# A shorter inverse root, a two-part transpose of z and two redistributed quarters of values in a hybrid attention and FFN kernel

## The chip, the cores and the metric

The kernel runs on one core of one Trainium2 chip. The metric is the device time of one execution in microseconds (us). Engines are named as in the profile: PE (TensorE matmul), PEld (its weight loads), DVE (VectorE), ACT (ScalarE), POOL (GpSimd), SP (SyncE, which here only issues DMAs). All data are fp32. The trace shows most fp32 matmuls as two records each, transposes as one.

## The reference

The input x is four images of 512 x 256. Four residual blocks follow one another, each on a layer norm of x:

```python
x = x + attn_a(layernorm(x))   # window attention on 16-channel tokens
x = x + ffn(layernorm(x))      # 256 -> 2048 -> 256, gated, weights stored as 4-bit codes
x = x + attn_b(layernorm(x))   # causal attention, 16 heads of 16, rope
x = x + ffn(layernorm(x))      # the same FFN weights
```

`attn_a` has two branches of 8 channels, each with attention in windows of 8 tokens, plus a depthwise convolution of the values ("lepe"); the two are joined, projected, normalised over 16 channels (with a weight and a bias) and added to the tokens. `ffn` first decodes its weights (a table of 16 values, one scale per 32), then computes `down(gelu(gate(x)) * up(x))`.

## The kernel before

**The passes.** The work goes image by image. Image 0's window attention runs alone at the start (the startup). Then image 0's first FFN pass runs on PE while DVE does image 1's window attention and decodes the remaining FFN weights (the first slot, `first_slot`). Then the FFN pass of image 1 runs beside the window attention of image 2, that of image 2 beside image 3 (`weave` with `beside_window`). Image 3's first pass and the second FFN passes follow, beside the causal attention. An FFN pass is 64 matmuls of 512 columns into gate banks (`pg`, L893) and up banks (`pu`, L914) and 64 of 256 columns into output banks (`po`, L939). Each of 16 hidden chunks needs one DVE product `it` (L923 in the first slot) before its `po` matmuls; each finished `po` bank is added to X by DVE (L954).

**What sets the order.** Each engine executes its own queue in order and waits on semaphores. In the startup and the first slot the order of PE and DVE is the order in which the program is written out (in the startup also ACT and SP). In the first slot a planner (`Pace`) decides where the FFN matmuls go between the window work: it keeps two clocks, `pe` and `dve`. `spend(us)` adds to the DVE clock and lets PE take further FFN steps (0.88 us each, two matmuls) as long as the PE clock is behind; it also emits FFN products and adds that have come due. `matmuls(us)` adds window matmuls to the PE clock. The planner only knows these written costs. In the later images only PE's order is by hand; DVE's is the scheduler's.

**Names around the change.**
- `window_front`: loads image b as `xa`, takes the variance of 128 rows (L323, L326), averages it over two halves with a small matmul `pm` (L295), gets a power -0.5 on POOL (L334), scales `xa` (L347 DVE, L351 ACT), transposes it (`yTp`, L360; copied by ACT to `yT`, L367), and makes the matmuls `qkv` (L408), `taps` (L393) and `lepe` (L381), which ACT copies to `T` (L419, L425). For image 0, `busy(n)` puts n matmuls on PE whose results nobody reads (`idle`, L451), 8 before `pm` and 12 after it.
- `window_parts`: `products` and `weighted` make 128 x 2048 products on DVE (`tq`, L517; `tv`, L598, L608). `values_here` folds such a product on DVE in three steps and adds lepe (L621, L623). `values_piled` instead accumulates its 8 slices on PE with identity matmuls (`va`, L478), and `take_piled` copies the bank by ACT into `att` (L639). `halved` does the first fold on DVE (L485), so that only 4 slices are left to pile. The buffers of `tmp` are two.
- `window_back`: `project(hf)` transposes half of `att` (`aTp`, L696), ACT copies it to `aT` (L698, one buffer), PE projects it (L702), DVE adds the bias (`pr`, L705), scales it (`prw`, L709) and sums the squares (`ss`, L711). `turn()` calls `newton_root` (L97 to L102) on `ss` and makes the two halves of `z` (L721, L723). `move()` brings both halves of `z` to row layout with 64 small matmuls (`zp`, L741), and `add()` adds them to X (L752).
- `norm_rows` then takes the row statistics (L828 to L834), POOL's power (L835), the scaled rows `xn` (L846), their transposes `xTp` (L866) and ACT's copies to `xT` (L869), with which the image's FFN pass starts.
- `dequant` (driven as `words`) loads the packed codes and scales of 12 weight quarters (`pkg`, `sbg` and so on; L780 to L783) and decodes each in six DVE steps (L797 to L810). In the startup `next(words)` after the statistics of image 0 sets off the first load: DVE writes one column of `pkg` (L780), and SP, whose queue holds all later loads, starts after it.

Of the kernel before, what the change touches and what calls it, by code (L numbers as in the profile page):

```python
# [10 lines left out]
F32 = mybir.dt.float32  # L11
# [3 lines left out]
ALU = mybir.AluOpType  # L15
AX = mybir.AxisListType

P = 128
# [17 lines left out]
def hybrid_kernel(  # L36
# [34 lines left out]
    def pair(name):  # L71
        return side.tile([P, 2, 512], F32, tag="pair", name=name)
# [21 lines left out]

    def newton_root(y, var, t, scale):

        nc.vector.tensor_scalar(var, var, scale, EPS, ALU.mult, ALU.add)  # L97
        nc.vector.tensor_scalar(y.bitcast(I32), var.bitcast(I32), -0.5, float(0x5F3759DF), ALU.mult, ALU.add)
        for _ in range(3):
            nc.vector.tensor_tensor(t, y, y, ALU.mult)  # L100
            nc.vector.scalar_tensor_tensor(t, t, -0.5, var, ALU.mult, ALU.mult)
            nc.vector.scalar_tensor_tensor(y, t, 1.5, y, ALU.add, ALU.mult)  # L102

    class Pace:

# [179 lines left out]
    def window_front(a1, a2, c, b, y, state):  # L285
# [12 lines left out]
        if b in (1, 2):  # L298

            junk = a1.tile([P, P], F32, tag="junk", name=f"junka{b}")  # L300
            for s in range(8):
                if b == 2 and s == 4:
                    yield 2.5
                nc.scalar.activation(junk, y[:, s, :], AF.Identity, accum_out=mv[:, s, 0:1])
            yield 3.5
            ps = over_halves(0, mv[:, :, 0])
            nc.scalar.activation(mean, ps, AF.Copy, scale=-1.0 / P)
            yield 1.0
            for s in range(8):
                if b == 2 and s == 4:  # L310
                    yield 2.5
                nc.scalar.activation(
                    junk, y[:, s, :], AF.Square, bias=mean[:, s : s + 1], accum_out=mv[:, s, 1:2]
                )
            yield 3.5
            nc.scalar.activation(off, over_halves(1, mv[:, :, 1]), AF.Copy, scale=1.0 / P)
            inv_root(rs, off)
            nc.gpsimd.tensor_tensor(mean, mean, rs, ALU.mult)
            yield 3.0
        else:  # L320
            for s in range(8):
                st = a2.tile([P, 6], F32, tag="st", name=f"sta{b}_{s}")
                ins = nc.vector.bn_stats(st, y[:, s, :])  # L323
                if b == 3:
                    queue_behind(ins, state["f1"])
                nc.vector.bn_aggr(mv[:, s, :], st)  # L326
            yield 3.5
            if b == 0:
                busy(8)
            mm = over_halves(0, mv.rearrange("p s t -> p (s t)")).rearrange("p (s t) -> p s t", t=2)  # L330
            nc.vector.tensor_tensor(off, mv[:, :, 0], mm[:, :, 0], ALU.subtract)
            nc.vector.tensor_tensor(off, off, off, ALU.mult)
            nc.vector.scalar_tensor_tensor(off, off, EPS, mm[:, :, 1], ALU.add, ALU.add)
            nc.gpsimd.tensor_tensor(rs, off, mhalf, ALU.pow)  # L334

            yield 4.0
            yield 4.0
            behind = last_on(mybir.EngineType.DVE).name
            ins = nc.vector.scalar_tensor_tensor(mean, mm[:, :, 0], -1.0, rs, ALU.mult, ALU.mult)
            if b > 1:  # L340
                queue_behind(ins, behind)
# [339 lines left out]
    def window_back(a1, a2, c, b, state):  # L681


        y, att = state[b]
        attf = att.rearrange("p s j c -> p s (j c)")
        ss = a1.tile([P, 2, 32], F32, tag="ss", name=f"ss{b}")

        prs = a1.tile([P, 4, 8, 64], F32, tag="tmp", bufs=2, name=f"prw{b}")
        prs = [prs[:, 2 * hf].rearrange("p a n -> p (a n)").rearrange("p (n c) -> p n c", c=C) for hf in range(2)]

        def project(hf):
            n = f"{b}_{hf}"
            pss = pair(f"aTp{n}")
            ps = pss[:, 0, :]
            for s in range(4):
                nc.tensor.transpose(ps[:, s * P : (s + 1) * P], attf[:, 4 * hf + s], ident)  # L696
            aT = a1.tile([P, 4, P], F32, tag="aT", name=f"aT{n}")
            nc.scalar.copy(aT.rearrange("p s q -> p (s q)"), ps)  # L698
            yield 1.2
            ps = pss[:, 1, :]  # L700
            for s in range(4):
                nc.tensor.matmul(ps[:, s * P : (s + 1) * P], aT[:, s, :], c["pw"], start=True, stop=True)  # L702
            yield 0.0
            pr = a2.tile([P, 32, C], F32, tag="pr", name=f"pr{n}")
            nc.vector.tensor_tensor(pr, ps.rearrange("p (n c) -> p n c", c=C), bcast(c["pb"], 1, 32), ALU.add)  # L705
            paced(0.6)
            sq = a2.tile([P, 32, C], F32, tag="sq", name=f"sqa{n}")
            nc.scalar.activation(sq, pr, AF.Square)
            nc.vector.tensor_tensor(prs[hf], pr, bcast(c["lnw"], 1, 32), ALU.mult)  # L709
            paced(0.6)  # L710
            nc.vector.tensor_reduce(ss[:, hf], sq, AX.X, ALU.add)  # L711
            paced(0.6)
            yield 1.8

        def turn():
            root = a1.tile([P, 2, 64], F32, tag="root", name=f"root{b}")
            newton_root(root[:, 0], ss.rearrange("p a n -> p (a n)"), root[:, 1], 1.0 / C)
            zs = []
            for hf in range(2):
                pr = prs[hf]  # L720
                nc.vector.tensor_tensor(pr, pr, bcast(root[:, 0, 32 * hf : 32 * hf + 32], 2, C), ALU.mult)  # L721
                z = a2.tile([P, 4, 4, 4, 8], F32, tag="sq", name=f"z{b}_{hf}")
                ins = nc.vector.tensor_tensor(  # L723
                    z.rearrange("p c i s j -> p (s j) i c"),
                    pr.rearrange("p n (i c) -> p n i c", c=4),
                    y[:, 4 * hf : 4 * hf + 4].rearrange("p s (j i c) -> p (s j) i c", j=8, c=4),
                    ALU.add,
                )
                zs.append(z)
            state[b, "z"], state[b, "moved"] = zs, ins.ins.name  # L730
            yield 7.2

        def move():


            ps = state[b, "moving"] = pair(f"zp{b}")
            for hf in range(2):
                z = state[b, "z"][hf]
                for q in range(8):
                    for c4 in range(4):  # L740
                        nc.tensor.matmul(  # L741
                            ps[32 * c4 : 32 * c4 + 32, q // 4, (q % 4) * P : (q % 4 + 1) * P],
                            c["sel"][:, q, hf, :],
                            z[:, c4].rearrange("p i s j -> p (i s j)"),
                            start=hf == 0 and q % 4 == 0,
                            stop=hf == 1,
                            skip_group_check=True,
                        )

        def add():  # L750
            to = X[b].rearrange("p i (s q j) -> p (i s) q j", s=4, q=8)
            ins = nc.vector.tensor_tensor(  # L752
                to, to, state[b, "moving"].rearrange("p a n -> p (a n)").rearrange("p (q n j) -> p n q j", q=8, j=8), ALU.add
            )
            state["due"] = ins.ins.name

        return project, turn, move, add


# [548 lines left out]
    def drain(work):  # L1308
        for _ in work:
            pass  # L1310
# [37 lines left out]
    with ExitStack() as left:  # L1348
# [21 lines left out]
        with tc.manual_schedule(  # L1370
            engines={mybir.EngineType.PE, mybir.EngineType.DVE, mybir.EngineType.Activation, mybir.EngineType.SP}
        ):
            wconst = next(consts)
            front = window_front(a1, a2, wconst, 0, xa, state)
            next(front)
            next(words)
            next(consts)
            next(front)
            next(consts)
# [34 lines left out]
            next(ahead)  # L1414
            rows_shift(wconst, 0)
            w["weighted"](0, 1)
            w["lepe_first"](1)
            w["values_piled"](0, 1)
            w["total_here"](1)
# [25 lines left out]
            add()  # L1445
            busy(1, wconst["wide"])
            drain(ahead)
            busy(2, wconst["wide"])
            drain(norm_rows(f1, 0, "f0", got, aside=lambda: some(words, 3)))
            del state["due"]  # L1450

# [4 lines left out]
        def first_slot():  # L1456
# [45 lines left out]
            for br in range(2):  # L1502
# [4 lines left out]
                for hf in range(2):  # L1507
                    w["weighted"](br, hf)
                    if br == 0:
                        step()  # L1510
                    if (br, hf) == (1, 0):
                        w["values_piled"](br, hf, one("va1"))
                        run.matmuls(4.2)
                        w["take_piled"](br, (hf,))
                        continue
# [15 lines left out]
            run.matmuls(0.9)  # L1531
            drain(second)
            pieces(72 - made[0])
            drain(turn())
            run.spend(6.2)
            while run.steps < 89:
                run.spend(0.2)
            move()
            run.matmuls(3.8)
            run.spend(max(0.0, run.pe - run.dve))  # L1540
            add()
            run.spend(1.2)
# [154 lines left out]
```

## Time and profile before

| what | value |
|---|---|
| three runs, us | 1021.25, 1021.71, 1024.87 (median 1021.71) |
| the profiled execution, us | 1020.95 |
| its span, us (1.85 us lie around it) | 1019.1 |
| PE busy in the span | 1000.8 us (98%) |
| DVE busy | 672.2 us (66%) |
| ACT, POOL busy | 350.8 us, 128.1 us |
| startup: 0 to 72.9 us | PE busy 65.71 |
| first slot: 72.9 to 182.0 us | PE busy 103.89 |
| the rest: 182.0 to 1019.0 us | PE busy 831.17 |
| granted TensorE clock, mean | 0.996 |

The busy share of PE counts matmuls whose results nobody uses, and a matmul at half the clock counts twice as long. What PE waits for is read in two views: the timeline of PE, which puts idle time and what ended it in brackets behind a line, and the stretches, which give busy time and granted clock for any interval. Times there are us from the start of the span.

### The profile page before, as it was taken

What the parts mean: (1) busy time and instruction counts of PE and PEld (TensorE: products, weight loads), DVE (VectorE), ACT (ScalarE), POOL (GpSimd) and SP (SyncE); (2) the same over time, 40 slices, a digit from 0 to 9 for tenths busy, and PEclk for the clock granted to TensorE, in tenths of its full rate; (3) what the DMA queues carried; (4) which work ended last, traced back from release to release, by engine and by line L of the source; (5) the groups of instructions that cost most, each with busy time, mean ns of one, the idle gap of its engine ahead of it and who ended that gap; (6) DMA issues with size and microseconds to landing.
All of it is one profiled execution on the core that took longest, in us unless ns stands there. A gap on an engine that the chain in (4) does not pass through costs nothing.

```text
span 1019.1 us, 14265 instructions
## 1 busy us (share of the span) xinstructions
PE 1000.8 (98%) x5548; PEld 590.8 (58%) x5548; DVE 672.2 (66%) x1591; ACT 350.8 (34%) x606; POOL 128.1 (13%) x251
## 2 busy tenths in 40 slices
PE   8999998999999999999999999999999999999998
PEld 6864667465746575554574644754645746446556
DVE  8889998887948678756577554766466575652111
ACT  3463241133112223435424346145253253451110
POOL 2100000100000013012330112401113201120000
PEclk9999999899999999999999999999999999999999
DMA  5220100000000020000000000000000000000000
GB/s 148 85 62 23 62 22 22 0 1 1 1 1 0 2 68 1 1 1 1 1 2 0 2 1 1 6 16 1 1 1 1 21 1 2 1 1 21 0 1 21
DMA packets 14900, 15.32 MB, mean 15 GB/s; under 512 B 2866, under 2 KB 11338, under 8 KB 14802
## 3 DMA queue, kind: packets, MB, share of 16 engines
q1 hardware_dynamic: 12416, 13.31, 4.4%
q10 hardware_dynamic: 2322, 1.07, 0.5%
q8 instruction: 43, 0.70, 0.3%
q14 instruction: 23, 0.19, 0.1%
q0 software_dynamic: 96, 0.05, 0.0%
HBM read 12.32 MB, written 2.10 MB: 14 GB/s over the span
## 4 chain that ended last, share of the span: by engine, by line
PE 93%; DVE 4%; DMA 1%; POOL 0%; ACT 0%; issue 0%; POOLq 0%; SPq 0%; DVEq 0%; ACTq 0%
PE pg_s L893 11%; PE pg_f L893 11%; PE pu_s L914 11%; PE po_f L939 11%; PE pu_f L914 11%; PE po_s L939 11%; PE s L1103 5%; PE o L1188 4%; PE sT L1152 4%; PE qkv_b L1042 3%; PE va L478 1%; PE zp L741 1%; PE qkT L1079 1%; PE qkv_b L1046 1%; PE sc L478 1%; PE ob L1203 1%
## 5 line engine op out<-in xcount | busy, mean ns | idle before, releaser
L1118 DVE CUSTOM_DVE_ANT_0 junk<-s,mask 128x512 f32<-128x512 f32 (+3 forms) x256 | 110.1, 486 | 36.9 <-PE s L1103 19.8
L893 PE MATMUL pg_f<-xT_f,g 128*128 128x512 f32 x256 | 125.6, 606 | 1.4 <-ACT xT_f L869 1.3
L893 PE MATMUL pg_s<-xT_s,g 128*128 128x512 f32 x256 | 126.7, 603 | 0.0
L914 PE MATMUL pu_s<-xT_s,u 128*128 128x512 f32 x256 | 125.4, 601 | 0.0
L914 PE MATMUL pu_f<-xT_f,u 128*128 128x512 f32 x256 | 122.6, 596 | 0.0
L939 PE MATMUL po_s<-d,it_s 128*128 128x256 f32 x512 | 118.0, 382 | 0.0
L939 PE MATMUL po_f<-d,it_f 128*128 128x256 f32 x512 | 117.0, 381 | 0.0
L939 PEld LDWEIGHTS po_s<-d,it_s 128*128 128x128 f32 x512 | 95.2, 190 | 20.8 <-issue 8.8
L939 PEld LDWEIGHTS po_f<-d,it_f 128*128 128x128 f32 x512 | 95.2, 190 | 18.0 <-issue 5.6
L1168 POOL TENSOR_SCALAR_AFFINE_SELECT e<-e 128x256 f32<-128x256 f32 x128 | 52.5, 422 | 344.9 <-ACT e L1164 342.3
L1164 ACT ACTIVATE e<-sT 128x1024 f32<-128x1024 f32 (+1 forms) x72 | 66.4, 968 | 72.0 <-PE sT L1152 72.0
L914 PEld LDWEIGHTS pu_f<-xT_f,u 128*128 128x128 f32 x256 | 47.4, 191 | 55.1 <-issue 52.4
L893 PEld LDWEIGHTS pg_s<-xT_s,g 128*128 128x128 f32 x256 | 45.9, 190 | 56.8 <-issue 50.9
L893 PEld LDWEIGHTS pg_f<-xT_f,g 128*128 128x128 f32 x256 | 47.3, 192 | 54.2 <-issue 48.1
L914 PEld LDWEIGHTS pu_s<-xT_s,u 128*128 128x128 f32 x256 | 46.1, 190 | 54.4 <-issue 50.2
L905 ACT ACTIVATE gs_f<-pg_f 128x512 f32<-128x512 f32 x48 | 28.6, 596 | 128.7 <-PE pg_f L893 125.8
L902 DVE SCALAR_TENSOR_TENSOR g_s<-g_s,gs_s 128x512 f32<-128x512 f32 x48 | 33.2, 691 | 59.0 <-ACT g_s L901 58.5
L899 ACT COPY gs_s<-pg_s 128x512 f32<-128x512 f32 x48 | 28.1, 586 | 67.8 <-PE pg_s L893 67.5
L1103 PE MATMUL s<-kT,qT 16*128 16x384 f32 (+3 forms) x512 | 50.0, 467 | 0.0
L954 DVE TENSOR_TENSOR X<-po_s,X 128x256 f32<-128x256 f32 (+1 forms) x33 | 13.5, 412 | 54.0 <-PE po_s L939 54.0
L1188 PE MATMUL o<-e,V 128*32 128x256 f32 (+3 forms) x512 | 44.4, 441 | 0.3 <-PE sT L1152 0.3
L1103 PEld LDWEIGHTS s<-kT,qT 16*128 16x128 f32 x512 | 23.1, 183 | 32.5 <-issue 11.6
(236 smaller groups left out, 1348.6 us busy)
## 6 DMA issues: line engine op xcount, KB each, us to landing
X<-in_x_dram SPq DMA_DIRECT2D x4, 512.0 KB
out_dram<-X SPq DMA_DIRECT2D x15, 128.0 KB
xa<-in_x_dram SPq DMA_DIRECT2D x28, 64.0 KB
pkg<-in_gate_p_dram SPq DMA_DIRECT2D x4, 256.0 KB
sbg<-in_gate_s_dram SPq DMA_DIRECT2D x4, 256.0 KB
pku<-in_up_p_dram SPq DMA_DIRECT2D x4, 256.0 KB
sbu<-in_up_s_dram SPq DMA_DIRECT2D x4, 256.0 KB
pkd<-in_down_p_dram SPq DMA_DIRECT2D x4, 256.0 KB
```

The lines of the kernel that those rows point to most:

```text
L893: nc.tensor.matmul(pg, Wf["g"][par][q][:, o : o + P], xT[:, par, :], start=par == 0, stop=par == 1)
L902: nc.vector.scalar_tensor_tensor(g2, g2, 1.0, gs, ALU.add, ALU.mult)
L905: nc.scalar.activation(gs, pg, AF.Gelu_apprx_tanh)
L914: nc.tensor.matmul(pu, Wf["u"][par][q][:, o : o + P], xT[:, par, :], start=par == 0, stop=par == 1)
L939: nc.tensor.matmul(po[:, 0:W], inter[k][:, i * P : (i + 1) * P], Wf["d"][par][j // 2][:, (j % 2) * W : (j % 2 + 1) * W], start=k == 0, sto ...
L1042: nc.tensor.matmul(ps[:, 0, :], xT[:, par, rows], c["wqk"][:, :, par], start=par == 0, stop=par == 1)
L1103: nc.tensor.matmul(pss[hl // 2][:, hl % 2, at : at + n], qT[h0 : h0 + HD, g, i * P : (i + 1) * P], kT[h0 : h0 + HD, g, 0:n], start=True, s ...
L1118: nc.vector.tensor_tensor_reduce(out=junk[:, 0:n], in0=pss[k][:, hl % 2, at : at + n], in1=c["mask"][:, 512 - n : 512], scale=1.0, scalar= ...
L1152: nc.tensor.matmul(pss[hl // 2][:, hl % 2, at : at + n], kT[h0 : h0 + HD + 1, g, kt * P : (kt + 1) * P], qT[h0 : h0 + HD + 1, g, kt * P : ...
L1164: nc.scalar.activation(e[:, :, 0 : 512 - at0], pss[k][:, :, at0:512], AF.Exp)
L1168: nc.gpsimd.affine_select(out=diag, in_=diag, pattern=[[0, 2], [1, P]], compare_op=ALU.is_ge, fill=0.0, base=0, channel_multiplier=-1,)
L1188: nc.tensor.matmul(outs[g][h0 : h0 + 32, kt * P : 512], v[:, kt, 4 * g + hl, :], e[:, hl % 2, at : at + n], start=kt == 0, stop=kt == 2,)
```

## The change

Seven edits, in the order in which they take effect:

1. **Earlier first load.** Image 0's first `next(words)` (the one-column write and SP's load behind it) is put between the fourth and the fifth row statistic instead of behind all eight.
2. **Idle matmuls.** `busy(8)` ahead of `pm` becomes `busy(14)`; the last `busy(2)` of the startup becomes `busy(1)`.
3. **Startup values.** The product of branch 0, half 1 is halved by DVE, and PE piles 4 slices instead of 8.
4. **`aT` in two buffers.**
5. **`newton_root`.** The variance is scaled by 64/9 in the instruction that adds epsilon; after the bit-trick seed, one cubic step (four instructions) and one Newton step (three) replace three Newton steps of three instructions: nine instructions instead of eleven. All images use it.
6. **First slot, values.** Branch 0, half 0 of image 1 is no longer folded on DVE alone: DVE halves it, PE piles 4 slices and lepe, ACT copies the bank to `att`.
7. **First slot, z.** `turn()` yields after each half, and `move` takes the halves it is to move. In the first slot the program now reads: first half of z, `spend(4.0)`, move half 0, second half of z, `spend(1.8)`, move half 1. The rule that FFN step 89 had to be reached first is gone.

Edits 6 and 7 change the planner's clocks, so it puts the FFN matmuls elsewhere. In the queue of PE as built, the second matmul of the last up chunk and all of the second half's `po` matmuls come behind the projections of image 1: that `pu` matmul, 8 `po` of the first output bank, 4 of the second, the two halves of `zp` side by side, then 10 `po`, the first four `xTp`, 2 `po`, the other four `xTp` and 8 `po`. Before, PE made 8 of the 32 `po` matmuls around `yTp` and `qkv`, 18 between the projections and `zp`, and 6 behind `zp`. In DVE's queue the last product `it` (chunk 15), which stood behind `values_here` of half 0, now stands behind the first half of `z`; behind it comes the add of the first `po` bank, and then the second half of `z`.

```diff
     def newton_root(y, var, t, scale):
-        nc.vector.tensor_scalar(var, var, scale, EPS, ALU.mult, ALU.add)
+        over = 64.0 / 9.0
+        nc.vector.tensor_scalar(var, var, scale * over, EPS * over, ALU.mult, ALU.add)
         nc.vector.tensor_scalar(y.bitcast(I32), var.bitcast(I32), -0.5, float(0x5F3759DF), ALU.mult, ALU.add)
-        for _ in range(3):
-            nc.vector.tensor_tensor(t, y, y, ALU.mult)
-            nc.vector.scalar_tensor_tensor(t, t, -0.5, var, ALU.mult, ALU.mult)
-            nc.vector.scalar_tensor_tensor(y, t, 1.5, y, ALU.add, ALU.mult)
+        nc.vector.tensor_tensor(t, y, y, ALU.mult)
+        nc.vector.tensor_tensor(t, t, var, ALU.mult)
+        nc.vector.scalar_tensor_tensor(t, t, -10.0 / 3.0, t, ALU.add, ALU.mult)
+        nc.vector.scalar_tensor_tensor(y, t, 5.0, y, ALU.add, ALU.mult)
+        nc.vector.tensor_tensor(t, y, y, ALU.mult)
+        nc.vector.scalar_tensor_tensor(t, t, -0.5 / over, var, ALU.mult, ALU.mult)
+        nc.vector.scalar_tensor_tensor(y, t, 1.5, y, ALU.add, ALU.mult)
...
+                if b == 0 and s == 4:
+                    state["early"]()
                 ins = nc.vector.bn_stats(st, y[:, s, :])
...
-                busy(8)
+                busy(14)
...
-            aT = a1.tile([P, 4, P], F32, tag="aT", name=f"aT{n}")
+            aT = a2.tile([P, 4, P], F32, tag="aT", name=f"aT{n}")
...
+            state["early"] = lambda: next(words)
             next(front)
-            next(words)
...
             w["weighted"](0, 1)
+            w["halved"]("v", 0, 1)
             w["lepe_first"](1)
...
-            busy(2, wconst["wide"])
+            busy(1, wconst["wide"])
             drain(norm_rows(f1, 0, "f0", got, aside=lambda: some(words, 3)))
...
+                    if (br, hf) == (0, 0):
+                        w["halved"]("v", br, hf)
+                        w["values_piled"](br, hf, one("va0"))
+                        run.matmuls(2.4)
+                        w["take_piled"](br, (hf,))
+                        step()
+                        continue
...
-            drain(turn())
-            run.spend(6.2)
-            while run.steps < 89:
-                run.spend(0.2)
-            move()
-            run.matmuls(3.8)
+            turned = turn()
+            next(turned)
+            run.spend(4.0)
+            move((0,))
+            run.matmuls(1.9)
+            drain(turned)
+            run.spend(1.8)
+            move((1,))
+            run.matmuls(1.9)
```

## The prediction

> **What bounds the kernel now.** I read the head of the page and its chain first: PE is the bound.
>
> ```profile
> PE 1000.8 (98%) x5548; PEld 590.8 (58%) x5548; DVE 672.2 (66%) x1591; ACT 350.8 (34%) x606; POOL 128.1 (13%) x251
> PE 93%; DVE 4%; DMA 1%; POOL 0%; ACT 0%; issue 0%; POOLq 0%; SPq 0%; DVEq 0%; ACTq 0%
> ```
>
> Behind 182 us PE is busy 831.2 of 837.0 us, and its queue there stays the same. So the change can only act by the moment at which image 1's FFN pass starts (`pg_f` at 182.04), and by PE's clock around it. Next, the timeline of PE before that moment; brackets hold the idle time and what ended it.
>
> ```profile
> 157.78 0.66 PE L696 MATMUL aTp<-ident,att 128*128 128x128 f32 x4 [0.46 <-ACT att L639]
> 159.11 1.16 PE L702 MATMUL aTp<-pw,aT 128*128 128x128 f32 x8 [0.68 <-ACT aT L698]
> ...
> 161.44 1.16 PE L702 MATMUL aTp<-pw,aT 128*128 128x128 f32 x8 [0.73 <-ACT aT L698]
> 162.43 7.93 PE L939 MATMUL po_f<-d,it_f 128*128 128x256 f32 x36
> 170.29 3.70 PE L741 MATMUL zp<-z,sel 128*32 128x128 f32 x128
> 173.93 2.86 PE L939 MATMUL po_f<-d,it_f 128*128 128x256 f32 x12
> 179.43 1.94 PE L866 MATMUL xTp_f<-ident,xn_f 128*128 128x128 f32 x8 [2.65 <-DVE xn_f L846]
> 182.04 3.77 PE L893 MATMUL pg_f<-xT_f,g 128*128 128x512 f32 x4 [0.68 <-ACT xT_f L869]
> 185.62 1.91 PE L914 MATMUL pu_f<-xT_f,u 128*128 128x512 f32 x4
> ```
>
> PE idles 5.2 us here, 2.65 of it behind `zp`. The four `pg_f` records at 182.04 take 3.77 us, the four behind them 1.91: the stretches (busy us of PE, PEld, DVE, ACT, POOL, then granted clock, DMA share, GB/s) say why.
>
> ```profile
> 178.80:185.70 6.90, 5.60 (x13) 3.15 (x14) 6.10 (x11) 1.07 (x2) 0.04 (x1) 0.51 0.00 0
> ```
>
> The clock was halved for 6.9 us behind the 2.65 us pause. That cost 1.9 us in `pg_f` (3.77 against 1.88) and 0.6 in `xTp` (1.94 against 1.32 at 70.89): 2.5 us. In the timeline of DVE I look for the product `it_f` that the last `po` matmuls need, and for the way to z:
>
> ```profile
> 143.73 0.68 DVE L923 TENSOR_TENSOR it_f<-pu_f,gs_f 128x512 f32<-128x512 f32 x1
> ...
> 160.38 0.69 DVE L705 TENSOR_TENSOR pr<-aTp,pb 128x512 f32<-128x512 f32 x1 [1.02 <-PE aTp L702]
> ...
> 168.46 1.06 DVE L723 TENSOR_TENSOR z<-prw,xa 128x512 f32<-128x512 f32 x1
> ...
> 174.06 1.22 DVE L752 TENSOR_TENSOR X<-X,zp 128x1024 f32<-128x1024 f32 x1 [2.31 <-PE zp L741]
> ```
>
> **Startup, worked out: -1.3 us.** The timeline of PE at its beginning:
>
> ```profile
> 7.08 0.61 PE L295 MATMUL pm<-mva,halves 128*128 128x16 f32 x2 [0.64 <-DVE pkg L780]
> 7.53 4.86 PE L451 MATMUL idle<-ident 128*128 128x128 f32 x24
> 12.22 1.04 PE L360 MATMUL yTp<-ident,xa 128*128 128x128 f32 x8
> ```
>
> *Idle matmuls.* The 24 records are 12 matmuls, 0.40 us each (the 4 records at 13.10 take only 0.61). Six more ahead of `pm`, less its idle 0.64, are up to +1.7 us, and +0.2 if the faster spacing comes in early. I take +1.2 (some of the six fast). The rows at 11.8 (DVE L347 done) show `yTp` was held by idle matmuls until 12.22, so 0.4 is absorbed; `yTp`, the copies to T and the first `tq` come 0.85 later (bounds -0.1 and +1.3).
>
> *Earlier load.* The chain shows the `sbg` transfer (issued 8.43, 6.85 us) freeing DVE L810 at 15.37. It moves 1.55 us ahead, with all loads behind it on SP. But `tq` at 16.58 also waits for ACT's copies to T (end 16.48): worth nothing, as those are now later still. If a later load delayed the small constants, it would show as idle DVE ahead of 8.2; their issues (POOL by 3.8, ACT by 8.4) keep their place, so I price that at nothing.
>
> *Halving.* PE saves 4 matmuls of 0.4325 us (36 `po` records, 18 such matmuls, span 7.8) = 1.73. DVE pays 1.13 (L485 at 18.90), but its waits for `va` (0.77 and 1.99 us at 41.08 and 45.42) go, since the shorter pile frees the `tmp` buffer. With DVE running without a break from `tv` at 36.6: halving to 39.95, L578 to L590 to 42.3, four L608 (1.135 each) to 46.85, folds and L623 (2.86) to 49.75, instead of 50.68: -0.9. PE comes out alike, 0.85 - 1.73 = -0.9. What is late next is both.
>
> *Two aT buffers* remove 0.73 us of PE idle at 53.14, but `yT`'s copy stands behind ACT's second square, so that path gains only 0.9. *Root:* two of eleven instructions of 0.254 us (56.60 to 59.39) = -0.5. z's first half moves 1.4, `lepe`'s end 0.9; `zp` starts at about 60.0 instead of 61.32: **-1.3**. From there to `pg_f` at 72.89 everything is a chain behind `zp`. One fewer idle matmul only lengthens a pause that exists. Bounds by the idle matmuls: -2.2 to -0.8.
>
> **First slot, worked out: +0.7 us without clock effects, times before the startup's shift.** Until 141.33 (first `pu` matmul of chunk 15) the queues agree. Then PE piles 5 matmuls (2.16 us, to 143.5), `yTp` to 144.4, and waits for ACT's `yT` copy, about 1.2, because the `po` matmuls that filled this are gone; `qkv` starts at 145.6 (before 145.74), and the window matmuls end at 151.85. DVE drops two L621 and L623 (142.21 to 143.73, 1.52 us) and the last `it_f` (0.6): 2.1 ahead, so `va` no longer waits. It runs 3.89 to 155.75; with the three ACT hand-overs as before the first projection ends at 158.7, `pr` starts at 158.85 instead of 160.38. From `pr` to the end of z's first half took 9.15 us; without the X add (0.33) and two root instructions (0.5) it takes 8.3: 167.2 instead of 169.5.
>
> Here is the catch. PE, through with the second projection at 161.0, does `pu` (0.86) and seven `po` (3.03) until 164.9. The eighth needs product 15, which now stands **behind z's first half** on DVE: done 167.85. PE stands still for 3 us, and everything else waits behind that matmul: `zp`, and on DVE the add of the first bank, and behind that the second half of z. Then 5 `po` (2.16) to 170.1 and `zp` (3.64) to 173.75: X's add starts at 173.95 instead of 174.06. What z gained is gone; the two halves of `zp`, side by side in the queue, win nothing. After the add, DVE and POOL need 5.4 us as before (174.06 to 179.43). PE fills it with 10 `po` (4.33) and idles 1.2; two more `po` and the last eight hide ACT's copy (the 0.68 goes). The sum: from 179.3, `xTp` 0.9+0.1, ten `po` 4.33: `pg_f` at 184.6. Before, it came at 182.04 and lost 1.9 to the clock: as good as 183.9. So **+0.7**. Errors: each hand-over 0.1, together 0.5 either way.
>
> *The new pause's clock.* Nothing here shows a 3 us pause, only 2.65 (halved after it) and scattered 0.46 to 0.73 (157 to 161.5, not halved). Ends: nothing, and half of 6.9 us under full load, 3.4. The nearest row lost 2.5 with PE partly idle. I take **2.0**. The Trainium skill, "TensorE: Matmul & The Clock Gate", section "What's actually happening", says that the clock halves after at least one idle window of about 3.4 us and returns after a busy one: by that rule 3 us would not do it and the sum would be 1020.4. The 2.65 us here contradict that threshold. By its window length a single window at half speed would cost 1.7.
>
> *Later images.* The root is 0.5 us shorter on DVE, hidden under PE's full queue: nothing; without that cover 0.5 each.
>
> **Sum.** -1.3 + 0.7 + 2.0 = +1.4 on the profiled 1020.95 (span 1019.1 plus 1.85): 1022.35, so 1022.4. That execution lay 0.8 below the median of the three runs, 1021.71, so I expect about the same median: a change of 0.1%.
>
> **Rivals.**
> - *The clock holds* (pause split so that it isn't noticed). For: the pauses around 158 did not halve it. Against: 2.65 us did. -1.3 + 0.7: 1020.4; with the best startup 1019.4.
> - *The wait for product 15 isn't there*, because PE arrives later than I think. For: a product used to be ready 20 us early. Against: three DVE rows and eight PE matmuls in a fixed order. 3 us and the clock loss go: 1017.4.
> - *Slower:* the clock stays halved through the 15 us of PE work from the pause to `pg_f`, as `po`, `zp` and the second pause (1.2 us) follow. Each us at half clock costs 0.5. Four 3.4 us pieces (6.9 halved) cost 6.8: 1027.2. It decides from 11.4 us halved on (1026.1). Against: before, a partly busy 6.9 us was enough to get it back.
> - *It doesn't do what it says:* the two moves of z stand side by side in PE's queue; that this part wins nothing is already in the forecast.
>
> **Numbers.** Forecast 0.58, clock holds 0.27, no wait 0.06, slower 0.07, other 0.02. Range 1019.0 to 1025.5: from the second case's better half to the forecast with 3.4 for the clock and the worst startup (1024.3) and some 1.2 for a second short halving. Half a per cent, 5.1 us, is about what a measurement of this kernel can tell from no change. Faster than that would need nearly all pauses named here to go; I give it the other 0.02 and a third of the no-wait case: 0.04. Slower is the third rival: 0.07. Same is the rest: 0.89.
>
> **What would show it.** In the profile after: an idle bracket of 2.5 to 3.2 us ahead of a `po_f` line, put down to DVE `it_f` L933; `zp` near 169; `pg_f` of image 1 behind eight `po` without a bracket; no 3.77 us `pg_f`; a stretch near 167 to 172 at a lower clock; image 0's first `pg_f` near 71.6. It would be wrong if that bracket is missing or under 1 us, or if the startup does not shorten.

## The result, and the profile after

The changed kernel took **1023.02 us** (median of 20 runs, 1019.75 to 1025.52), the kernel before 1021.73 us beside it (20 runs, 1019.44 to 1025.21): ratio 1.0005, 95% interval 0.9992 to 1.0017. No difference can be measured. The profiled execution took 1019.76 us (span 1018.0).

The page's line of busy time and the chain of what ended last, of the changed kernel:

```profile
PE 997.9 (98%) x5560; PEld 589.5 (58%) x5560; DVE 670.6 (66%) x1581; ACT 351.2 (34%) x607; POOL 128.6 (13%) x251
PE 94%; DVE 4%; ACT 1%; POOL 1%; issue 0%; POOLq 0%; DVEq 0%
```

PE is the bound as before. The timeline of PE at startup:

```profile
8.49 0.29 PE L301 MATMUL pm<-mva,halves 128*128 128x16 f32 x2
8.64 2.92 PE L459 MATMUL idle<-ident 128*128 128x128 f32 x24
12.07 1.43 PE L368 MATMUL yTp<-ident,xa 128*128 128x128 f32 x8 [0.51 <-ACT xa L359]
...
69.01 1.32 PE L876 MATMUL xTp_f<-ident,xn_f 128*128 128x128 f32 x8 [1.28 <-DVE xn_f L856]
71.00 1.98 PE L903 MATMUL pg_f<-xT_f,g 128*128 128x512 f32 x4 [0.68 <-ACT xT_f L879]
```

Image 0's first `pg_f` comes at 71.00 instead of 72.89. `pm` is 1.4 later, but the twelve idle matmuls behind it (24 records) take 2.92 instead of 4.86, so `yTp` is not late. Ahead of `xTp` the idle time has grown from 0.43 to 1.28. Now PE in the first slot:

```profile
143.74 1.15 PE L416 MATMUL qkv<-bw,yT 32*128 32x96 f32 x32 [1.10 <-ACT yT L375]
...
159.20 1.02 PE L924 MATMUL pu_f<-xT_f,u 128*128 128x512 f32 x2
160.06 3.19 PE L949 MATMUL po_f<-d,it_f 128*128 128x256 f32 x14
166.13 2.42 PE L949 MATMUL po_f<-d,it_f 128*128 128x256 f32 x10 [2.88 <-DVE it_f L933]
168.48 3.70 PE L751 MATMUL zp<-z,sel 128*32 128x128 f32 x128
172.11 4.58 PE L949 MATMUL po_f<-d,it_f 128*128 128x256 f32 x20
177.62 0.67 PE L876 MATMUL xTp_f<-ident,xn_f 128*128 128x128 f32 x4 [0.92 <-DVE xn_f L856]
...
182.88 1.88 PE L903 MATMUL pg_f<-xT_f,g 128*128 128x512 f32 x4
```

The 2.65 us bracket ahead of `xTp_f` has become 0.92, but a new one of 2.88 stands ahead of the eighth `po`, put down to `it_f`, and one of 1.10 ahead of `qkv`. `pg_f` follows without a bracket and takes 1.88: in this execution, unlike in most runs, the clock is full throughout (granted 1.000). The timeline of DVE shows why the 2.88:

```profile
164.51 1.04 DVE L731 TENSOR_TENSOR z<-prw,xa 128x512 f32<-128x512 f32 x1
165.38 0.69 DVE L933 TENSOR_TENSOR it_f<-pu_f,gs_f 128x512 f32<-128x512 f32 x1
166.86 0.42 DVE L964 TENSOR_TENSOR X<-po_f,X 128x256 f32<-128x256 f32 x1 [0.79 <-PE po_f L949]
167.21 0.68 DVE L729 TENSOR_TENSOR prw<-prw,root 128x512 f32<-128x512 f32 x1
167.92 1.07 DVE L731 TENSOR_TENSOR z<-prw,xa 128x512 f32<-128x512 f32 x1
```

Product 15 stands behind z's first half, and an X add that waits for PE stands between the halves.

The times come in steps, and the steps are the clock: the four runs at granted clock 1.000 took 1019.75 to 1019.85, two at 0.998 took 1021.1, seven at 0.997 or 0.996 1021.9 to 1023.1, seven at 0.995 or 0.993 1023.6 to 1025.5. So two questions were open: does the pause of product 15 eat z's gain, and is it the pause that halves the clock?

### The profile page after: what moved, and what is told of

It reads as the page before. It is cut to its first block, busy times and chain, and to the rows that moved or that the text cites. A ratio compares the mean times of both kernels' runs of the same rounds, so it can differ in the third digit from the quotient of the medians.

```text
span 1018.0 us, 14278 instructions
## 1 busy us (share of the span) xinstructions
PE 997.9 (98%) x5560; PEld 589.5 (58%) x5560; DVE 670.6 (66%) x1581; ACT 351.2 (34%) x607; POOL 128.6 (13%) x251
## 4 chain that ended last, share of the span: by engine, by line
PE 94%; DVE 4%; ACT 1%; POOL 1%; issue 0%; POOLq 0%; DVEq 0%
PE pg_s L903 11%; PE pu_s L924 11%; PE pg_f L903 11%; PE po_s L949 11%; PE pu_f L924 11%; PE po_f L949 10%; PE s L1113 5%; PE o L1198 4%; PE sT L1162 4%; PE qkv_b L1052 3%; PE va L486 2%; PE zp L751 1%; PE qkT L1089 1%; PE qkv_b L1056 1%; PE sc L486 1%; PE ob L1213 1%
## 5 line engine op out<-in xcount | busy, mean ns | idle before, releaser
L1113 PEld LDWEIGHTS s<-kT,qT 16*128 16x128 f32 x512 | 23.1, 183 | 32.5 <-issue 11.6
```

Of the source, the lines that this page charges most:

```text
L1113: nc.tensor.matmul(pss[hl // 2][:, hl % 2, at : at + n], qT[h0 : h0 + HD, g, i * P : (i + 1) * P], kT[h0 : h0 + HD, g, 0:n], start=True, s ...
```

## The experiments

Every one ran beside the kernel before on its chip, whose median there was 1021.1 to 1021.7.

**1. Half of the change at a time.** *startup_only* leaves the two edits of the first slot out of the changed kernel (its main lines follow; the planner's calls around the moves are as before too). *slot_only* makes the same two edits alone in the kernel before:

```diff
-                    if (br, hf) == (0, 0):
-                        w["halved"]("v", br, hf)
-                        w["values_piled"](br, hf, one("va0"))
...
-            move((0,))
-            run.matmuls(1.9)
-            drain(turned)
...
-            move((1,))
...
+            drain(turn())
...
+            move()
```

> The changed startup and the shorter root alone; the first slot as before the change (both halves of z, then one move behind 36 records of po). Theory (the startup wins 1.9 us and all of it reaches the end; the first slot of the change gives it back): image 1's first pg_f 1.9 us earlier than before, median about 1019.8 us, with the same 2.65 us pause ahead of xTp and the same spread of the times. Rival (the startup's gain is absorbed by a wait of the first slot, so that the slot's part of the change cost nothing): median within 0.5 us of before, 1021.7.

Measured: 1019.90 us (12 runs, 1018.01 to 1024.56), ratio 0.9991 (0.9978 to 1.0004); its profile has the 2.65 us pause again. Its interval takes in no change. At equal clock the gain is clearer: its three runs at 0.998 took 1018.0 to 1018.3, those of the kernel before at 0.998 on that chip 1019.5 to 1021.3. So the startup's gain reaches the end, at least 1.2 us of it. In its profile `pg_f` of image 1 does not come 1.9 earlier, as expected, but at 182.66 (before 182.04): the clock was halved at 37.95 and at 72.09, in the startup.

> The two edits of the first slot alone (a quarter of values by both engines, z moved in two parts), with the startup and the long root of before. Theory: product 15 stands behind z's first half, which comes 0.5 us later with the longer root; the pause ahead of the eighth po is 3.3 to 3.5 us, and the median is 3 to 4 us above before, 1024.7 to 1025.7. Rival (the slot's part is neutral, startup gains absorbed): within 0.5 us of before.

Measured: 1030.21 us (6 runs, 1027.80 to 1033.04), ratio 1.0087 (1.0068 to 1.0106). PE's timeline:

```profile
145.68 1.15 PE L409 MATMUL qkv<-bw,yT 32*128 32x96 f32 x32 [1.10 <-ACT yT L368]
146.65 1.23 PE L394 MATMUL qkv<-taps,yT 32*128 32x32 f32 x40
147.81 3.56 PE L382 MATMUL lepe<-bl,yT 128*128 128x64 f32 x16
...
173.43 2.42 PE L942 MATMUL po_f<-d,it_f 128*128 128x256 f32 x10 [3.40 <-DVE it_f L926]
```

The pause is 3.40, as worked out, but the time is 5 us over what I expected. `lepe` takes 3.56 us (2.00 elsewhere): the clock is at a half from 147.97 to 158.21, **behind the 1.10 us wait for yT**, not behind the pause. No run had a clock above 0.995. I had not expected this.

**2. The pause filled.** Ahead of the eighth `po`:

```diff
+                    if later and half == 1 and i == 0 and k == 7:
+                        state[1, "moving"] = pair("zp1")
+                        for _ in range(3):
+                            nc.tensor.matmul(state[1, "moving"][:, 0], ident, state["wide"], start=True, stop=True)
```

> The changed kernel with three idle matmuls of 128x512 (0.86 us each) ahead of the eighth po of image 0's second half, written to the bank that zp overwrites; the work around keeps its place. Theory (the 2.9 us pause of PE is what draws the halved clock): all runs near 1019.8 us, granted clock 1.000, no spread of the times. Rival (the clock drops come from elsewhere, the startup or the chip): median 1023.0 and a spread from 1019.8 to 1025.5 as without them.

Measured: 1021.68 us (12 runs, 1019.67 to 1026.99), ratio 1.0005 (0.9987 to 1.0023); four runs at clock 1.000, eight at 0.998 to 0.992. The pause is 0.32 and the spread is still there: **my theory that the pause halves the clock fell.** The stretches of this kernel (busy us of PE, PEld, DVE, ACT, POOL, granted clock, DMA share, GB/s), cut where the clock changed:

```profile
142.91:146.32 3.41, 2.31 (x73) 2.07 (x71) 3.27 (x6) 1.01 (x1) 0.00 (x0) 1.00 0.00 0
146.32:149.74 3.42, 3.42 (x30) 3.38 (x26) 3.25 (x4) 1.84 (x4) 0.00 (x0) 0.50 0.00 0
149.74:153.15 3.41, 3.41 (x56) 3.29 (x58) 3.41 (x4) 0.59 (x1) 0.00 (x0) 0.50 0.02 5
153.15:156.56 3.41, 3.41 (x33) 2.98 (x30) 2.87 (x5) 1.84 (x4) 0.00 (x0) 0.50 0.00 0
156.56:159.98 3.42, 3.42 (x9) 2.70 (x9) 0.00 (x0) 0.00 (x0) 0.00 (x0) 0.50 0.00 0
```

Four pieces at half clock follow the stretch with the yT wait. It isn't empty (2.31 busy), but what runs in it are transposes and `qkv` matmuls that use 32 of the 128 rows. With one more at 37.10 they account for the 7.3 us by which this execution's span (1025.3) stands above 1018.0. Before the change, `po` matmuls filled this wait.

**3. Product 15 early.** The last `pu` matmul goes behind `yTp`, and its product behind att (0,1):

```diff
+                    if (br, hf) == (0, 1):
+                        next(run.main)
+                        run.steps += 1
+                        run.pe += run.each
...
+            run.room(0)
             next(first)
```

> The changed kernel with the last pu matmul of chunk 15 issued behind yTp (in the wait for ACT's yT copy) and product 15 put on DVE behind att (0,1), so that no po waits for it. Theory (product 15 behind z's first half is what cost the slot its gain): no idle bracket ahead of a po, zp starts at z's first half near 165.6, with 2.2 us idle ahead of it; X's add near 169.4 instead of 172.25; image 1's first pg_f near 180.0; span 1015.2 and time 1017.0 with the clock at 1.000, and some runs 1 to 3 us more if a pause of 2.2 us halves the clock too. Rival (z in two moves wins nothing whatever the product does, since DVE and POOL are late): 1019.8 to 1023.0 as without it.

Measured: 1018.15 us (12 runs, 1017.09 to 1021.96), ratio 0.9974 (0.9961 to 0.9987); the two runs at clock 1.000 have a span of 1015.4, expected 1015.2. Its profile (startup 0.6 later than in the changed kernel's, through a halved piece at 37):

```profile
159.81 5.35 PE L949 MATMUL po_f<-d,it_f 128*128 128x256 f32 x24
166.30 3.85 PE L751 MATMUL zp<-z,sel 128*32 128x128 f32 x128 [1.15 <-DVE z L731]
...
180.86 1.88 PE L903 MATMUL pg_f<-xT_f,g 128*128 128x512 f32 x4
```

No `po` waits any more, `zp` waits for z itself (1.15, where I had put 2.2), and `pg_f` is 2.0 earlier (2.6 without the 0.6). At clock 1.000 the times differ by 2.7 (1017.1 against 1019.8). That **product 15 ate z's gain** is shown.

**4. A new theory of the clock, and its test.** In the profiles so far all stretches of one clock, but for the last, are whole multiples of 3.413 us (before: 49, 2 and 244 of them; fill_pause: 9, 1, 31, 4 and 254), counted from the first full clock. So I took the clock to be set anew in each piece (the expectations say window) of a fixed grid, by what PE did in the piece before. First pieces of the kernel before, then of startup_only, with the same columns:

```profile
158.36:161.77 3.41, 2.00 (x16) 1.70 (x16) 2.29 (x5) 1.56 (x3) 0.00 (x0) 1.00 0.00 0
175.42:178.84 3.42, 1.36 (x7) 0.86 (x5) 2.16 (x9) 0.00 (x0) 1.01 (x1) 1.00 0.28 76
178.84:182.25 3.41, 2.15 (x9) 1.78 (x10) 3.38 (x6) 0.84 (x2) 0.00 (x0) 0.50 0.00 0
182.25:185.66 3.41, 3.41 (x5) 1.33 (x6) 2.72 (x6) 0.23 (x1) 0.00 (x0) 0.50 0.00 0
```

```profile
68.67:72.08 3.41, 1.76 (x10) 0.80 (x8) 3.41 (x7) 1.48 (x4) 0.79 (x1) 1.00 0.62 166
72.08:75.50 3.42, 3.11 (x4) 1.51 (x5) 3.32 (x5) 3.31 (x11) 0.00 (x0) 0.50 0.43 141
```

In before the piece with 1.36 busy is followed by half clock, the one with 2.00 is not. In startup_only the piece with 1.76 is; it holds the wait ahead of image 0's `xTp`, 1.28 long since the change. (Busy time is a rough measure, since the ends of matmuls are modelled: by the time in which their columns stream, two passes per record at the full clock, the three pieces are used to 35, 44 and 33%.) Sliding the grid over the changed kernel's trace, pieces as empty as these can fall in five places: 36 (`taps`, 32-row matmuls, and a 0.69 wait), 54 (yT), 66 (`xTp`), 143 (yT) and 164 (product 15). Of these, before has only the first; it has two others, the pause at 177 and, seldom, the wait ahead of `zp` at 61. *five_filled* is fill_pause with four more idle fillings:

```diff
             drain(front)
+            busy(1, wconst["wide"])
...
             busy(2, wconst["wide"])
+            busy(1, wconst["wide"][:, 0:384])
...
             drain(ahead)
-            busy(1, wconst["wide"])
+            busy(2, wconst["wide"])
...
+                    if (br, hf) == (0, 1):
+                        busy(1, wconst["wide"])
```

> The changed kernel with idle matmuls in all five places where its PE is little used: 36 (behind taps), 54 (the wait for yT at startup), 66 (two wide ones ahead of xTp, as before the change, instead of one), 143 (the wait for yT in the first slot) and 164 (the wait for product 15). The order of the work stays. New theory (the clock is set in windows of 3.41 us on a grid that starts with the first full clock; one in which PE streams less than some 36 to 40 per cent of the time, narrow matmuls counting less, is followed by one at half clock; where the grid falls is chance): no window is that empty any more, all runs at clock 1.000, 1019.6 to 1020.3 us without spread. Rival (a single long pause, or the chip, decides): the spread of 1019.7 to 1027 stays, as it did with the pause of product 15 filled alone.

Measured: 1019.42 us (12 runs, 1018.98 to 1020.45), ratio 0.9983 (0.9974 to 0.9992), all runs at 0.999 or 1.000; the kernel before, beside it on the same chip, ranged from 1019.0 to 1024.6 as ever. With matmuls that compute nothing, and no work moved, the spread went from 5.8 to 1.5 us, and the median lies 3.6 under the changed kernel's. What the theory forecast came true, and neither the chip nor a single long pause explains it. What may be left of the spread is the startup's place on the grid (not shown): the first full clock came between 6.1 and 8.8 us in the profiles with fourteen idle matmuls.

The same for the kernel before, *before_filled*:

```diff
             drain(front)
+            busy(1, wconst["wide"])
...
+            busy(1)
             move()
...
+            fills = [3]
             for _ in norm_rows(f1, 1, "f1", got, aside=lambda: run.spend(2.0)):
                 run.spend(0.45)
+                if fills:
+                    busy(fills.pop(), wconst["wide"])
```

> The kernel before the change with idle matmuls in its three little-used places: 36 (behind taps), 61 (one narrow, ahead of zp) and 177 (three wide ones in the 2.65 us pause ahead of xTp). Theory (windows of 3.41 us decide the clock): clock 1.000 in nearly all runs, 1018.8 to 1019.6 us, so that at the full clock the kernel before is 0.5 to 1 us faster than the changed one with its five places filled (1019.4). Rival (the kernel before loses its clock elsewhere): the spread of 1019.0 to 1024.6 stays.

Measured: 1018.64 us (10 runs, 1018.23 to 1019.50 and one of 1021.16 at clock 1.000, which stays unexplained), ratio 0.9975 (0.9964 to 0.9985). Its pause is gone, and `pg_f` takes 1.98:

```profile
71.05 1.32 PE L866 MATMUL xTp_f<-ident,xn_f 128*128 128x128 f32 x8 [0.43 <-DVE xn_f L846]
...
176.78 2.74 PE L451 MATMUL idle<-sel,ident 128*128 128x512 f32 x6
179.59 1.31 PE L866 MATMUL xTp_f<-ident,xn_f 128*128 128x128 f32 x8
181.58 1.98 PE L893 MATMUL pg_f<-xT_f,g 128*128 128x512 f32 x4 [0.68 <-ACT xT_f L869]
```

So at full clock the change costs some 0.8 us. The two intervals overlap, but the profiles' spans (1016.9 and 1017.8, both at clock 1.000) say the same, and so do the few unfilled runs at clock 1.000: 1018.8 to 1019.7 for the kernel before (four, beside these experiments), 1019.75 to 1019.85 for the changed one. The clock takes about 3 us from each: 2.9 by the medians from the kernel before, 3.6 from the changed one.

**5. The slot laid out anew.** *slot_filled* puts the slot's own `po` into its waits:

```diff
+                    if (br, hf) == (0, 1):
+                        release()
+                        run.hold = True
+                        put(1)
...
+                        put(1)
                         next(first)
...
+            release()
+            run.hold = True
+            put(1)
             next(first)
...
             next(second)
...
+            put(1)
             next(first, None)
             next(second)
...
             drain(second)
...
+            put(14)
             turned = turn()
             next(turned)
...
             move((0,))
...
             drain(turned)
...
+            release()
+            run.hold = True
             move((1,))
...
             add()
...
+            fills = [12, 1]
...
+            for _ in norm_rows(f1, 1, "f1", got, aside=lambda: None):
+                put(fills.pop(0) if fills else 0)
```

put(n) issues n matmuls of the FFN (the first is the last `pu`, in yT's wait; all others are `po`), and between hold and release no product and no X add goes to DVE. The planner's calls in between (`spend`, `matmuls`) are gone, and it stops before the last `pu`. *all_filled* has the three startup fillings of five_filled as well.

> The changed kernel with the slot laid out anew: the last pu matmul in the wait for yT, product 15 on DVE in its wait ahead of pr, one po in each of three hand-overs to ACT, 14 po ahead of zp, 12 behind it, one between the xTp, the last two beside ACT's copy. Theory (the slot's waits of 6.7 us can all be filled with work that is there, and DVE's chain allows it): image 1's first pg_f near 176.3 instead of 182.9, span 1011.5 and time 1013.3 at clock 1.000; halved windows only in the startup, which the edit leaves, none to two of 1.5 us, median near 1014.5. Rival (DVE's chain to xn_f is late, PE waits for it): pg_f not below 179, 1016 to 1018.

> The same slot, and idle matmuls in the three places of the startup (36, 54, 66). New theory of the clock: all runs at clock 1.000, 1013.3 us with a spread under 1 us. Rival (the chip or something else draws the clock): spread of 3 us or more above the lowest run, as in the slot alone.

Measured: slot_filled 1015.10 us (6 runs, 1014.29 to 1016.41), ratio 0.9939 (0.9924 to 0.9955), clock 1.000 to 0.996; all_filled **1014.09 us** (6 runs, 1013.77 to 1014.35), ratio 0.9928 (0.9912 to 0.9944), all at 1.000. Both stand 0.6 to 0.8 above what I had expected, and all_filled beats both the changed kernel and the kernel before. PE's timeline of all_filled:

```profile
154.31 0.59 PE L949 MATMUL po_f<-d,it_f 128*128 128x256 f32 x2
154.94 0.66 PE L704 MATMUL aTp<-ident,att 128*128 128x128 f32 x4
155.43 0.60 PE L949 MATMUL po_f<-d,it_f 128*128 128x256 f32 x2
156.27 1.16 PE L710 MATMUL aTp<-pw,aT 128*128 128x128 f32 x8 [0.24 <-ACT aT L706]
...
159.53 6.21 PE L949 MATMUL po_f<-d,it_f 128*128 128x256 f32 x28
166.04 3.70 PE L751 MATMUL zp<-z,sel 128*32 128x128 f32 x128 [0.30 <-DVE z L731]
169.67 5.45 PE L949 MATMUL po_f<-d,it_f 128*128 128x256 f32 x24
...
177.37 1.96 PE L903 MATMUL pg_f<-xT_f,g 128*128 128x512 f32 x4
```

The brackets of the slot are 0.30 at most; `pg_f` comes 5.5 us earlier than in the changed kernel. I had worked out 176.3; 0.3 of the miss comes from this execution's later startup (first `pg_f` of image 0 at 71.33 instead of 71.00), the rest isn't taken apart.

**6. What the parts are worth without clock and waits**, each taken out of all_filled (1014.09): z moved at once with 18 `po` ahead and 8 behind; the first quarter of values on DVE alone; the old root (its lines as before the change); eight idle matmuls instead of fourteen. The edits of the first, second and fourth:

```diff
             put(14)
-            turned = turn()
-            next(turned)
-            move((0,))
-            drain(turned)
+            drain(turn())
...
+            put(4)
+            move()
...
-                    if (br, hf) == (0, 0):
-                        w["halved"]("v", br, hf)
-                        w["values_piled"](br, hf, one("va0"))
...
-                busy(14)
+                busy(8)
```

> The kernel with the slot laid out anew and the startup filled, but with z moved at once behind its second half (18 po ahead of zp, 8 behind it ahead of xTp). Theory (once nothing stands in its way, moving the first half early lets zp end sooner): zp starts at 167.3 instead of 166.0, X's add and image 1's first pg_f 1.3 us later, 1015.4 us against 1014.1. Rival (PE is the bound there, the order of po and zp is nothing): 1014.1, within 0.3.

Measured: 1015.22 us (6 runs, 1014.92 to 1015.80), ratio 0.9942 (0.9929 to 0.9955): 1.1 slower, near the 1.3 expected. PE now waits where the X add has come late:

```profile
166.76 3.70 PE L751 MATMUL zp<-z,sel 128*32 128x128 f32 x128
170.39 3.72 PE L949 MATMUL po_f<-d,it_f 128*128 128x256 f32 x16
175.90 0.41 PE L876 MATMUL xTp_f<-ident,xn_f 128*128 128x128 f32 x2 [1.79 <-DVE xn_f L856]
```

> The same kernel with the first quarter of values added up on DVE alone, as before the change, not halved on DVE and piled on PE. Theory (the chain to z is DVE's): 1.5 us more on DVE, of which its wait ahead of pr takes some 0.5, so 1.0 us later, 1015.1 us. Rival (PE is the bound of the slot, and the pile costs it 2.2 us): 1 to 2 us faster, 1012 to 1013.

Measured: 1016.44 us (5 runs, 1015.84 to 1017.18), ratio 0.9953 (0.9940 to 0.9966): 2.3 slower, where I had expected 1.0. About 1.5 of it is the clock, at 0.998 in every run (estimated from the 5.25 against 3.72 below). PE, 2.2 us of piling short, waits for DVE's next product, and that wait halves the clock under the pile behind it (5.25 instead of 3.72):

```profile
150.32 5.25 PE L486 MATMUL va<-tv,ident 128*128 128x256 f32 x16 [2.80 <-DVE tv L616]
```

> The same kernel with the root of before (three quadratic steps, two instructions more). Theory (the root is on the path to zp both in the startup and in the slot): 0.5 us each, together 1.0, 1015.1 us. Rival (hidden in one of the two): 0.5 or less.

Measured: 1014.92 us (5 runs, 1014.87 to 1015.20), ratio 0.9938 (0.9925 to 0.9951): 0.8 slower, near the 1.0 expected.

> The kernel with the slot laid out anew and the startup filled, with eight idle matmuls ahead of pm as before the change instead of fourteen. Theory (the six more cost nothing, since they bring the full clock one window of 3.4 us sooner and the twelve idle matmuls behind pm then take 2.9 us instead of 4.9): 0 to 0.5 us slower without them, 1014.1 to 1014.6. Rival, the step of the prediction (they hold yTp and the first tq up by 0.85 us): 0.85 faster, 1013.2.

Measured: 1014.12 us (5 runs, 1013.43 to 1014.28), ratio 0.9925 (0.9911 to 0.9938): no difference that can be measured. The reason I gave isn't shown, since in this profile the full clock came at 6.9 us with eight too. (These four ran on other chips than all_filled; the ratios, each against the kernel before on its own chip, give 1.4, 2.5, 1.0 and -0.3. The ratios' intervals are some 1.3 us wide either way, so these prices are rough.)

## Why the prediction came out as it did, step by step

The forecast, 1022.4 us and no change that can be measured, lies 0.6 from the median. Part of that is luck: the startup came 0.6 better than put and the clock 1.2 worse, and how often the clock is halved differs from run to run. Without the clock the sum was near: -1.3 + 0.7 on the profiled 1020.95 is 1020.4, and the runs at full clock took 1019.8. By its steps:

- **Startup, -1.3: measured -1.9, one term mis-sized.** The halving, the two aT buffers and the root came within some 0.3 us of what was worked out. The idle matmuls, put at 0.85 us for the first `tq`, cost 0.18 in the profile (before, then after):

```profile
16.58 2.28 DVE L517 TENSOR_TENSOR tq<-T 128x2048 f32<-128x2048 f32 x1
16.76 2.29 DVE L525 TENSOR_TENSOR tq<-T 128x2048 f32<-128x2048 f32 x1 [0.26 <-ACT T L427]
```

In the changed kernel's profile the full clock came at 8.2 us instead of 11.6, and the twelve behind `pm` took 2.9 us instead of 4.9. I had priced those at the old clock. Eight instead of fourteen changes the median by nothing that can be measured (eight_idle). Whether the six more bring the full clock sooner stays open: with eight it came at 11.4 and 11.6 in two profiles, at 6.7 and 6.9 in two.

- **The earlier load, "worth nothing": so only where the full clock comes late.** In before_filled, where it came at 6.7, ACT's copy for `tq` ended at 15.42, but `tq` started at 16.63, behind a decoding step that had waited 0.54 us for `sbg`. In eight_idle, with the earlier load and the full clock at 6.9, `tq` started at 16.00, 0.04 behind the copy. No run takes this edit out alone, so its worth isn't shown.
- **First slot without the clock, +0.7: right, term by term.** Less the startup's 1.9, I had the pause 3 us (2.88), `zp` at 168.2 (168.48), the X add at 172.05 (172.25), `pg_f` at 182.7 (182.88). The 0.7 counts before's halved stretch in. Against before_filled, at full clock, the slot takes 3.3 us more (`xTp` of image 0 to `pg_f` of image 1: 113.9 against 110.5). In product_early it takes 111.2, so the queueing of product 15 makes 2.6 of the 3.3; the other 0.7 isn't taken apart.
- **The new pause's clock, +2.0: too small, and the mechanism wrong.** The median lies 3.2 above the runs at full clock (1023.02 against 1019.8). "Nothing here shows a 3 us pause, only 2.65": I tied the loss to the longest pause. fill_pause took the pause away and the loss stayed; five_filled filled all five places and the loss went. In the profiled execution the 2.88 us pause halved nothing, and the stretch at a lower clock that I expected near 167 to 172 isn't there. Against the filled kernels, the changed one loses 3.6 us to the clock and the kernel before 2.9, where I had 2.0 and 2.5.
- **"`yT` copy, about 1.2"** (1.10): its length was right; that it could cost more than its length, up to four halved pieces, I didn't see.
- **"One fewer idle matmul only lengthens a pause that exists": wrong.** The pause grew from 0.43 to 1.28 us, and in startup_only the clock halved behind it.
- **The rivals.** "The clock holds" (1020.4) is what the profiled execution and three others in 20 show, at 1019.8. "Slower", the clock halved through several pieces, did occur (four in fill_pause), but behind the yT wait and not in the median. That the two moves of z win nothing side by side was right here, and is no property of the edit: with its way clear the same edit is worth 1.1 us.

## What to carry to other kernels

Where times spread in steps, look at the granted clock of every run first: compare kernels at the full clock, and price the clock by itself. Before work is taken out of a wait of PE, ask what is left in the few us around it; a short wait among narrow matmuls can cost more than a long one among wide ones, and an idle matmul there is worth its place. And when one thing is moved ahead in an in-order queue, look for what now stands behind it: the product here cost more than z's early half could win, and moving it, not the half, made the edit pay.

## What the runs showed of the hardware

- The clock of PE is granted in pieces of 3.413 us. In the 14 profiles every stretch of one clock, but for the last, is a whole number of them. The Trainium skill, "TensorE: Matmul & The Clock Gate", section "What's actually happening", gives a free-running window of 3413 ns: this agrees.
- The same section has the clock halved after at least one idle window. Here none of the windows ahead of a halved one was idle; in before PE was busy for 1.36 of the 3.41 us, in fill_pause for 2.31.
- What separates the pieces is how far PE is used. I add up from the records the time in which columns stream, overlapping records counted once, and count time in which only 32-row matmuls stream at 5/8 (a weight fitted afterwards, to the same profiles). Then the ten pieces that were followed by a first halved one, in the 14 profiles, lie at 35.5% or under, and all other pieces at full clock in the first 200 us at 37.5% or over (the emptiest of the product 15 pause in the changed kernel's profile: 38%). No kernel was made to test this bound by itself.
- By the same measure, with columns at half speed, the ten halved pieces behind which the full clock came back are used to 82% or more, and the seven behind which half clock went on to 67% or less. That PE looks busy says little: the piece at 149.74 of fill_pause, shown above, is busy throughout and used to 39%. So the clock is lost under two fifths of use and regained somewhere above two thirds.
- One halved piece (granted 0.998) cost 1.3 us of the whole time in the changed kernel (1021.1 against 1019.8) and 0.5 to 1.2 in slot_filled (1014.8 to 1015.5 against 1014.3).
